# Value steps applied to the head outputs, and gated biases prepared in the projections

## The chip, the cores and the metric

The kernel runs on one core of one Trainium2 chip. A core has a matrix engine (TensorE, PE in the profile), a vector engine (VectorE, DVE), a scalar engine (ScalarE, ACT), a general one (GpSimd, POOL) and a sync engine (SyncE, SP), which here does nothing but issue DMAs. Each engine takes its own instructions in order, and the engines wait for one another on semaphores. The metric is device time in microseconds (us), taken over one execution of the whole program.

## The reference

`x` is 4 x 512 rows of 512 numbers (2048 rows in all, 16 tiles of 128), the context is 4 x 1024 rows (4096 rows, 32 tiles). All query rows see all context rows: the batch is folded into one.

```
x = x + tanh(g_xattn) * xattn(layernorm(x), ctx)
x = x + tanh(g_ffn)   * ffn(layernorm(x))

xattn: q = xn @ Wq + bq ; k, v = ctx @ Wkv + bkv          (16 heads of 32)
       q, k rounded to 8-bit integers, one step for each row and head
       v rounded to 8-bit integers, one step for each column of v:  v = vint * sv[column]
       p = softmax(q k^T / sqrt(32)), rounded to 0..255, one step for each row
       o = p @ v ;  y = o @ Wp + bp
ffn:   two layers with ternary weights on 8-bit rows, silu, gelu and a layernorm between; bias b1, b2
```

`sv` has one number for each of the 512 columns of `v`, that is for each (head, column of the head). The columns of `o` are the rows of `Wp`, so the factor `sv` can be put on `v`, on `o` or on the rows of `Wp`. The tests draw biases that are not zero.

## The kernel before

**The projections** (the first 235 us or so). 48 steps, one for each row tile: 32 of the context and 16 of `x`, in an order written out by hand (`order`). A step turns a tile on TensorE, multiplies it by the weights and rounds the rows on VectorE. Beside them a dictionary `extra` holds work that is hung on a step number: the gates' loads (step 5), their `tanh` (step 45, `gates`), the loading of the FFN weights in eight pieces through two buffers of the pool `wr` (`piece_load`, `piece_sum`, `piece_ternary`, `piece_store`), and `b1` (steps 22 and 23). GpSimd has little to do here. SP issues every load and store of this stage in order.

**The attention.** 256 units, one for each (head, tile of 128 query rows). In unit i TensorE makes 4096 scores for each row, VectorE multiplies them by the keys' steps out of PSUM into a buffer and takes the row maximum, in three chunks of 1536, 1536 and 1024 (`scores`, line 731; a, b and c below). Then `exps(i)` runs: two tiny GpSimd instructions join the three maxima (`m`, line 746) and make the bias (`nb`, line 748), and ScalarE makes the exponentials as bytes (`r`, line 751). A DMA transposes `r` (`turn_exps`, line 765), GpSimd spreads the bytes to 16 bits in two casts for each unit (`rT`, line 785), and TensorE multiplies them with the integers of `v` (line 801). After four units of a head ScalarE takes the sum out of PSUM (`leave`, line 812) and its own queue stores it to `ods` (line 813). Program order puts `scores(i+1)`'s first chunk ahead of `exps(i)`.

There are three score buffers up to unit 237 (`TWO`); one of them, `third`, is then given up and holds `Wp` (`wp_sb`), the biases `bp` and `b2` (`vecs`) and `b1`. From there on two buffers are left, so that chunk a of unit i+2 can only start when `exp(i)` is done.

A dictionary `plan` holds work hung on (unit, place in the unit). The values of head groups 1, 2 and 3 (`plan_group`) are made inside the attention, in units 3 to 63, 64 to 128 and 129 to 193. The last heads' units also start the output projection: `load_for_ffn` at unit 239 loads `Wp` and the biases into `third`; GpSimd then puts the gate on `bp` (`vector_for_ffn`, line 190), the values' steps on the four blocks of `Wp` (`projection_step`, line 281), adds `bp` to the first two tiles of `x` (`bias_x`, line 1001) and puts the gate on `b2`. Tile 0 has its softmax steps widened on ScalarE (`wide_step`, line 1014) and turned on TensorE at unit 242, multiplied with `o` on VectorE at 243 (`scale_o`, line 1036), projected with `Wp` from 243 to 247 (`first_project`, line 1404) and added to `x` at 247 (`residual_x`, line 1049). Tile 1 does the same from unit 248 on.

**The FFN** (from 1450 us or so). Tiles go in pairs; each turn of the pipeline has TensorE, ScalarE, VectorE and GpSimd on different pairs. `bias_x` adds `bp` to the later tiles of `x`, and `bias_y` adds `b2`.

Of the kernel before, what the change touches and what calls it, by code (L numbers as in the profile page):

```python
# [33 lines left out]
def flamingo_kernel(  # L34
# [124 lines left out]
    }  # L159
    b1r = third[:, at_vecs + 8 * C : at_vecs + 8 * C + 2 * INNER].bitcast(BF16)  # L160
    b1d = dram.tile([3, INNER], BF16, name="b1d")

    def load_b1(pool):
        bf = pool.tile([IC, P], F32, name="bf", bufs=1)
# [11 lines left out]

    def load_for_ffn():
        nc.sync.dma_start(wp_sb, wp.rearrange("(c p) n -> p c n", p=P))
        for name, v in (("bp", bp), ("b2", b2)):
            nc.sync.dma_start(vecs[name], row(v, C))  # L180
        for r in range(2):
            for a in range(3):
                at = r * HD + 3 * a
                nc.sync.dma_start(
                    b1r[at : at + 3, :].rearrange("p (m n w) -> p m n w", n=2, w=512)[:, :, r, :],
                    b1d.rearrange("p (m n w) -> p m n w", n=2, w=512)[:, :, r, :],
                )

    def vector_for_ffn(name, tg):
        nc.gpsimd.tensor_scalar(vecs[name], vecs[name], tg, 0.0, ALU.mult, ALU.add)  # L190

    def key_tile(n):

# [82 lines left out]
            vqs[g] = vqp.tile([P, KT, P], F16, name="vq")  # L276
        nc.sync.dma_start_transpose(vqs[g][:, j * VB : (j + 1) * VB, :], vh)

    def projection_step(g):

        nc.gpsimd.tensor_scalar(
            wp_sb[:, g, :], wp_sb[:, g, :], sv[:, g : g + 1], 1.0 / INT_STEP, ALU.mult, ALU.mult
        )

    def integers(pool, f, scale):

# [21 lines left out]
    with tc.tile_pool(name="pw", bufs=1) as pw, tc.tile_pool(  # L308
# [215 lines left out]
            partial(nc.sync.dma_start, bq_sb, row(bq, C)),  # L524
        ]
        extra[5].append(load_gates)
        extra[45].append(gates)
        extra[4] += [partial(nc.vector.tensor_scalar, bq_sb, bq_sb, QSCALE, None, ALU.mult)]
        for j in range(8):
            extra[6 + 2 * j].append(partial(piece_load, j))  # L530
# [9 lines left out]

        extra[22].append(ffn_load)
        extra[23].append(lambda: parts_of_b1(pieces.pop(0), wr))
        LASTK = KT + QT - END - 1
        for k, n in ((-6, 0), (-3, 4), (-1, 5), (1, 1), (1, 2), (1, 3)):
            extra[LASTK + k].append(partial(load_piece, 0, n))
# [87 lines left out]
    def plan_group(g, u0, dense):  # L633
        wv_g = wvs.next()
        vmx = fs.tile([P, KT // VB], F32, name="vmx")
        state = {}

        def start(j):
            return u0 + 3 * j - min(j, dense)

        def values(b):
            if b in (0, 5, 6, 7):
                return vgs[b % 4]
            if g not in vqs:
                vqs[g] = vqp.tile([P, KT, P], F16, name="vq")
            at = (b - 1) * VB * P
            return vqs[g].rearrange("p a b -> p (a b)").bitcast(F32)[:, at : at + VB * P]

        def load(j):
            cT = cTs.next()  # L650
            b, a = divmod(j * VW, VB * P)
            nc.sync.dma_start(cT, cTd[b][:, :, a : a + VW])
            state["cT", j] = cT

        def product(j, c):
            if c == 0:
                state["acc"] = aav.tile([P, 512], F32, name="vacc")[:, :VW]
            nc.tensor.matmul(  # L658
                state["acc"], wv_g[:, c, :], state["cT", j][:, c, :],
                start=(c == 0), stop=(c == CC - 1),  # L660
            )

        def leave(j):
            b, a = divmod(j * VW, VB * P)
            nc.scalar.activation(  # L665
                values(b)[:, a : a + VW],
                state.pop("acc"),
                AF.Identity,
                bias=bv[:, g : g + 1],
            )  # L670
            state.pop(("cT", j))

        def largest(b):
            nc.vector.tensor_reduce(
                vmx[:, b : b + 1], values(b), AX.X, ALU.max, apply_absolute_value=True
            )

        def integer(j):
            state["vi", j] = value_integers(vis.next(), g, values(j))

        def cast(j):
            state["vh", j] = vhs.next()
            nc.vector.tensor_copy(state["vh", j], state.pop(("vi", j)))

        def turn(j):
            values_by_key(state.pop(("vh", j)), g, j)

        nc.sync.dma_start(wv_g, values_weight(g))
        load(0)
        for j in range(NV):  # L690
            u = start(j)
            v = start(j + 1) - 1
            for c, place in enumerate(((u, 2), (u + 1, 0), (v, 0) if v > u + 1 else (v, 1), (v, 2))):
                plan[place].append(partial(product, j, c))
            if j + 1 < NV:
                plan[u, 1].append(partial(load, j + 1))
            plan[v, 2].append(partial(leave, j))
            if (j + 1) * VW % (VB * P) == 0:
                plan[v + 1, 1].append(partial(largest, j * VW // (VB * P)))
        u = start(NV)  # L700
        plan[u + 1, 0].append(partial(value_scale, g, vmx))
        for k, j in enumerate((1, 0, *range(2, KT // VB))):
            n = u - 1 + 2 * k
            plan[n + 3, 0].append(partial(integer, j))
            plan[n + 4, 2].append(partial(cast, j))
            plan[n + 5, 1].append(partial(turn, j))
# [65 lines left out]
    def plan_values(i, h, tg):  # L772

        pTs = [heads.pop(("p", h, tg * TG // 2 + u)) for u in range(TG // 2)]
        acc = aav.tile([P, 512], F32, name="acc")[:, :P]
        vq = vqs[h // HPG]
        NW = KT // 2 // 4
        spreads = {}  # L780

        def spread(k, u, cast=nc.gpsimd.tensor_copy):
            if u == 0:
                spreads[k] = at.tile([P, TG, 2 * NW, P], F16, name="rT")
            cast(  # L785
                spreads[k][:, 2 * u : 2 * u + 2, :, :]
                .bitcast(I16)
                .rearrange("p a (two b) q -> p a two (b q)", two=2),
                pTs[u][:, :, k * NW : (k + 1) * NW, :]
                .rearrange("p a b q -> p a (b q)")  # L790
                .bitcast(U8)
                .rearrange("p a (n two) -> p a two n", two=2),
            )

        def products(k):
            rT = spreads.pop(k)
            for b in range(2 * NW):
                two, w = divmod(b, NW)
                kb = at_tile[two * KT // 2 + k * NW + w]
                for c in range(TG):  # L800
                    nc.tensor.matmul(  # L801
                        acc[c * HD : (c + 1) * HD, :],
                        vq[:, kb, h % HPG * HD : (h % HPG + 1) * HD],
                        rT[:, c, b, :],
                        start=(k == 0 and b == 0),
                        stop=(k == 3 and b == 2 * NW - 1),
                        tile_position=(0, c * HD),
                    )

        def leave():  # L810
            o = ar.tile([P, P], F32, name="o", bufs=2)
            nc.scalar.copy(o, acc)
            nc.scalar.dma_start(
                ods[tg][h * HD : (h + 1) * HD, :].rearrange("d (c q) -> c d q", c=TG), o
            )

        for k in range(4):
            for u in range(TG // 2):

                unit = i + 4 + k  # L820
                if unit < len(steps):
                    place = unit, 0
                else:
                    place = unit - 1, 2 + (unit == len(steps))
                plan[place].append(partial(spread, k, u))
            plan[i + 5 + k, 1].append(partial(products, k))
        plan[i + 8, 2].append(leave)
# [159 lines left out]
        return range(g * GT, (g + 1) * GT)  # L987

    def load_x(t):
        nc.sync.dma_start(X[t], x[t * P : (t + 1) * P, :])  # L990

    def load_o(t):
        o = fm["o"].next()
# [16 lines left out]
    def wide_step(t):  # L1010

        step_w = fm["step_w"].next()
        step = ff.pop(("step", t))
        nc.scalar.copy(step_w, step.unsqueeze(2).to_broadcast([P, H, HD]))
        ff["step_w", t] = step_w

    def bias_y(g):
# [381 lines left out]
    def first_project(t, n):  # L1399
# [6 lines left out]
            start=(k == 0), stop=(k == NG - 1),  # L1406
        )

    for j in range(8):
        a = j * INNER // 8  # L1410
        at_unit(
            199 + 3 * j, 1,
            partial(
                nc.sync.dma_start_transpose,
                w1T[:, :, a : a + INNER // 8],
                w1q[a : a + INNER // 8, :],
            ),
        )
    at_unit(TWO + 2, 0, load_for_ffn)
    at_unit(TWO + 3, 2, partial(vector_for_ffn, "bp", tg1))  # L1420
    for g in range(NG):
        at_unit(TWO + 4 + g // 2, 1, partial(projection_step, g))
    at_unit(TWO + 7, 1, partial(vector_for_ffn, "b2", tg2))
    at_unit(
        TWO + 7, 1,
        partial(
# [5 lines left out]
    for t in range(2):  # L1432
        at_unit(240, t, partial(load_x, t))
        at_unit(241, 1, partial(load_o, t))
        at_unit(242 + t, 0, partial(bias_x, t))
    at_unit(241, 0, partial(steps_x, 0))
    for t, u in ((0, 242), (1, 248)):
        at_unit(u - 1, 2, partial(wide_step, t))
# [181 lines left out]
```

## Time and profile before

| | |
|---|---|
| median of 3 runs | 1698.74 us (1696.87 to 1700.41) |
| the profiled execution | 1701.51 us |
| its span in the trace | 1699.7 us |
| instructions | 31473 |
| granted TensorE clock, mean | 0.651 of full speed |
| mean DMA rate | 178 GB/s |

Busy time counts the instructions of an engine, not its waits. The stages differ: TensorE is busy for nine tenths and more of the projections, VectorE for nearly all of the attention, with GpSimd not far behind, and no engine alone fills the FFN. So a change is read in the stage where it lies. The chain that ended last leads back through casts on GpSimd (8% of the span), score chunks on VectorE (3%) and many small links.

In the lines below the first number is the start in us from the start of the span and the second the duration, or the span of a merged group; what stands in square brackets is the idle time of the engine just before, and what ended it.

### The profile page before, as it was taken

The page shows a single profiled execution, that of the slowest core. Times are in us where ns is not written, and L with a number is a line of the kernel's source. Part 1 is how long each engine was busy: PE and PEld are TensorE (multiplying, and loading weights), DVE is VectorE, ACT ScalarE, POOL GpSimd, SP SyncE. Part 2 cuts the span into 40 slices and gives each one's busy share as a digit, 9 for nine tenths or more (in the row PEclk, how much of TensorE's full clock was granted, in tenths as well). Part 3 has the DMA queues.
Part 4 walks back from the last instruction along what each step waited for, and adds up shares of the span by engine and source line. Part 5 has one row for each costly group of instructions (what it writes and reads, how often), then busy time and mean ns, then how long its engine had stood idle before and what let it go on. Part 6 is the DMA issues. An engine that isn't in the chain of part 4 may idle for free. (4 is left out here: it accounts for less than half of the span.)

```text
span 1699.7 us, 31473 instructions
## 1 busy us (share of the span) xinstructions
PE 1352.5 (80%) x12174; PEld 589.7 (35%) x12174; DVE 1564.2 (92%) x2205; ACT 1346.5 (79%) x988; POOL 1284.0 (76%) x1315
## 2 busy tenths in 40 slices
PE   8999968888966889986689898666665676789986
PEld 4444423333322333332233333222222233334432
DVE  5787889999999999999999999999999989588987
ACT  2443468888889888888988888898887876679987
POOL 0001226999999999999989999999999998566645
PEclk9999975565555555565555555555555556899998
DMA  6767969999999999998899999889999776613325
GB/s 210 273 249 249 295 196 222 196 212 207 159 180 171 217 178 209 199 170 177 158 211 185 207 197 178 180 151 189 173 183 174 153 139 128 171 43 87 93 50 117
DMA packets 729418, 303.32 MB, mean 178 GB/s; under 512 B 657266, under 2 KB 702902, under 8 KB 722870
## 3 DMA queue, kind: packets, MB, share of 16 engines
q1 hardware_dynamic: 720502, 296.60, 81.6%
q10 hardware_dynamic: 8736, 4.72, 1.1%
q8 instruction: 95, 1.56, 0.4%
q14 instruction: 53, 0.43, 0.1%
q0 software_dynamic: 32, 0.01, 0.0%
HBM read 103.86 MB, written 33.83 MB: 81 GB/s over the span
## 5 line engine op out<-in xcount | busy, mean ns | idle before, releaser
L785 POOL CAST rT<-pT 128x2048 int16<-128x2048 uint8 x506 | 944.5, 1893 | 22.9 <-issue 5.6
L731 DVE CUSTOM_DVE_ANT_0 s<-ps_s,skb 128x1536 f32<-128x1536 f32 x531 | 805.6, 1574 | 15.3 <-PE ps_s L722 7.5
L751 ACT ACTIVATE r<-s,nb,sq 128x4096 uint8<-128x4096 f32 x177 | 673.8, 3807 | 118.3 <-POOL nb L748 96.2
L722 PE MATMUL ps_s<-kT,qT 32*128 32x512 bf16 x2048 | 458.3, 585 | 264.5 <-DVE m L731 250.1
L731 DVE CUSTOM_DVE_ANT_0 third<-ps_s,skb 128x1536 f32<-128x1536 f32 (+1 forms) x237 | 362.6, 1574 | 3.8 <-ACT r L751 1.3
L751 ACT ACTIVATE r<-third,nb,sq 128x4096 uint8<-128x4096 f32 x79 | 300.7, 3806 | 47.8 <-POOL nb L748 35.9
L722 PEld LDWEIGHTS <-qT 32*128 32x128 bf16 x2048 | 97.7, 98 | 591.0 <-issue 581.9
L801 PE MATMUL acc<-rT,vq 128*32 128x128 f16 x8192 | 262.6, 305 | 19.4 <-POOL rT L785 9.9
L801 PEld LDWEIGHTS <-vq 128*32 128x32 f16 x8192 | 195.4, 137 | 131.5 <-issue 106.9
L658 PE MATMUL vacc<-fx 128*128 128x256 f32 x384 | 227.8, 695 | 2.6 <-ACT vq L665 1.9
L746 POOL TENSOR_SCALAR m<-m 128x1 f32<-128x1 f32 x256 | 91.9, 359 | 60.4 <-DVE m L731 50.7
L471 POOL TENSOR_SCALAR nsq<-sq 128x16 f32<-128x16 f32 x16 | 3.2, 203 | 171.7 <-DVE sq L290 171.7
L658 PEld LDWEIGHTS vacc<-fx 128*128 128x128 f32 x384 | 93.5, 302 | 83.9 <-issue 80.5
L430 PE MATMUL kacc<-wk_sb,cT 128*128 128x512 f32 x256 | 117.6, 603 | 0.0
L748 POOL TENSOR_SCALAR nb<-m,nsq 128x1 f32<-128x1 f32 x256 | 68.0, 266 | 23.9
L1113 PE MATMUL ph<-fx,skb 128*128 128x512 bf16 x256 | 63.6, 393 | 0.1
L430 PEld LDWEIGHTS kacc<-wk_sb,cT 128*128 128x128 f32 x256 | 47.1, 194 | 47.6 <-issue 46.9
L731 DVE DVE_READ_ACCUMULATOR2_ANT m<- 128x1 f32 x768 | 63.0, 82 | 0.0
L430 PE MATMUL qacc<-wq_sb,xT 128*128 128x512 f32 x128 | 59.4, 608 | 0.1
L459 DVE TENSOR_TENSOR f<-kacc,bk_sb 128x512 f32<-128x512 f32 x32 | 22.0, 689 | 30.9 <-PE kacc L430 29.9
L299 ACT COPY cT<-tr 128x512 f32<-128x512 f32 x32 | 18.6, 581 | 34.6 <-PE tr L298 34.4
L359 POOL TENSOR_SCALAR wi<-wt 128x512 bf16<-128x512 int32 (+1 forms) x32 | 21.7, 703 | 31.5 <-ACT wt L355 31.5
(236 smaller groups left out, 1365.4 us busy)
## 6 DMA issues: line engine op xcount, KB each, us to landing
skb<-skd SPq DMA_DIRECT2D x32, 1024.0 KB
fx<-cTd SPq DMA_DIRECT2D x48, 512.0 KB
wt<-in_L_ffn_w_dram SPq DMA_DIRECT2D x16, 1024.0 KB
in<-in_ctx_dram SPq DMA_DIRECT2D x32, 256.0 KB
cTd<-cT SPq DMA_DIRECT2D x8, 1024.0 KB
q4d<-rows4q SPq DMA_DIRECT2D x16, 512.0 KB
pT<-r SPq DMA_TRANSPOSE x260
in<-in_x_dram SPq DMA_DIRECT2D x16, 256.0 KB
```

Of the source, the lines that this page charges most:

```text
L359: nc.gpsimd.tensor_scalar(wi[:, a : a + w4], wt.bitcast(I32)[:, a : a + w4], 1.0, -1.0, ALU.min, ALU.max)
L430: nc.tensor.matmul(acc, tT[:, c, :], wk_sb[c] if kind == "k" else wq_sb[:, c, :], start=(c == 0), stop=(c == CC - 1),)
L459: nc.vector.tensor_tensor(f, acc, bk_sb, ALU.add)
L658: nc.tensor.matmul(state["acc"], wv_g[:, c, :], state["cT", j][:, c, :], start=(c == 0), stop=(c == CC - 1),)
L722: nc.tensor.matmul(ps_s[:, b * KB - k0 : (b + 1) * KB - k0], qT[rows, 0, t * P : (t + 1) * P], kT[rows, 0, a * KB : (a + 1) * KB], start=True,
L731: nc.vector.tensor_tensor_reduce(s[:, k0 : k0 + w], ps_s[:, :w], skb[:, k0 : k0 + w], 1.0, -3.0e38, ALU.mult, ALU.max, m3[:, n : n + 1],)
L746: nc.gpsimd.tensor_scalar(m, m3[:, 0:1], m3[:, 1:2], m3[:, 2:3], ALU.max, ALU.max)
L748: nc.gpsimd.tensor_scalar(nb, m, nsq[:, t, h : h + 1], LN255, ALU.mult, ALU.add)
L751: nc.scalar.activation(r.rearrange("p (n two) -> p two n", two=2), s.rearrange("p (two n) -> p two n", two=2), AF.Exp, bias=nb, scale=sq[: ...
L785: cast(spreads[k][:, 2 * u : 2 * u + 2, :, :] .bitcast(I16) .rearrange("p a (two b) q -> p a two (b q)", two=2), pTs[u][:, :, k * NW : (k ...
L801: nc.tensor.matmul(acc[c * HD : (c + 1) * HD, :], vq[:, kb, h % HPG * HD : (h % HPG + 1) * HD], rT[:, c, b, :], start=(k == 0 and b == 0), ...
L1113: nc.tensor.matmul(ph[:, n, :], xqT[:, c, tok], w1T[:, c, at : at + 512], start=(c == 0), stop=False,)
```

## The change

The step `sv` is no longer multiplied onto `Wp`. It is stored to memory for each group of four heads and read back with the head's column as the partition, repeated for the four row tiles that share the PSUM tile (`svr`); `leave` multiplies by it while it takes a sum out of PSUM. The constant that went with it is put on in `wide_step`. The gates' `tanh` is taken at step 9 of the projections instead of step 45. The two biases are gated there, added to the first two tiles of `x`, and stored to memory (`xbd`, `gbd`); later loads read these.

```diff
-        for name, v in (("bp", bp), ("b2", b2)):
-            nc.sync.dma_start(vecs[name], row(v, C))
+        for k, name in enumerate(("bp", "b2")):
+            nc.sync.dma_start(vecs[name], gbd[k : k + 1, :].broadcast_to([P, C]))
...
-    def vector_for_ffn(name, tg):
-        nc.gpsimd.tensor_scalar(vecs[name], vecs[name], tg, 0.0, ALU.mult, ALU.add)
...
-    def projection_step(g):
-
-        nc.gpsimd.tensor_scalar(
-            wp_sb[:, g, :], wp_sb[:, g, :], sv[:, g : g + 1], 1.0 / INT_STEP, ALU.mult, ALU.mult
-        )
+    svr = keep.tile([P, H], F32, name="svr")
+    svd = dram.tile([NG, P], F32, name="svd")
+
+    def store_scale(g):
+        nc.sync.dma_start(svd[g : g + 1, :].rearrange("a p -> p a"), sv[:, g : g + 1])
+
+    def load_scale(g):
+        for c in range(HPG):
+            nc.sync.dma_start(
+                svr[c * HD : (c + 1) * HD, g * HPG : (g + 1) * HPG],
+                svd[g : g + 1, :].rearrange("a (h d) -> (a d) h", d=HD),
+            )
...
-        extra[45].append(gates)
+        extra[9].append(gates)
...
+        def bias_load():
+            wt = wr.tile([P, INNER], F32, name="wt")
+            biased.append(wt)
+            for k, v in enumerate((x[:P, :], x[P : 2 * P, :], row(bp, C), row(b2, C))):
+                nc.sync.dma_start(wt[:, k * C : (k + 1) * C], v)
+
+        def bias_steps():
+            wt = biased[0]
+            for k, tg in ((2, tg1), (3, tg2)):
+                b_k = wt[:, k * C : (k + 1) * C]
+                nc.gpsimd.tensor_scalar(b_k, b_k, tg, 0.0, ALU.mult, ALU.add)
+            for k in range(2):
+                for a in range(0, C, P):
+                    x_k = wt[:, k * C + a : k * C + a + P]
+                    nc.gpsimd.tensor_tensor(x_k, x_k, wt[:, 2 * C + a : 2 * C + a + P], ALU.add)
+
+        def bias_store():
+            wt = biased.pop()
+            nc.sync.dma_start(
+                xbd.rearrange("(a p) c -> p a c", p=P),
+                wt[:, : 2 * C].rearrange("p (a c) -> p a c", c=C),
+            )
+            nc.sync.dma_start(
+                gbd.rearrange("(a k) c -> a k c", a=1),
+                wt[:1, 2 * C :].rearrange("p (a c) -> p a c", c=C),
+            )
+
+        for k, f in ((21, bias_load), (22, bias_steps), (24, bias_store)):
+            extra[k].append(f)
...
+        plan[u + 2, 2].append(partial(store_scale, g))
+        plan[u + 5, 2].append(partial(load_scale, g))
...
-            nc.scalar.copy(o, acc)
+            nc.scalar.activation(o, acc, AF.Identity, scale=svr[:, h : h + 1])
...
-        nc.sync.dma_start(X[t], x[t * P : (t + 1) * P, :])
+        src = xbd if t < 2 else x
+        nc.sync.dma_start(X[t], src[t * P : (t + 1) * P, :])
...
-        nc.scalar.copy(step_w, step.unsqueeze(2).to_broadcast([P, H, HD]))
+        nc.scalar.activation(
+            step_w, step.unsqueeze(2).to_broadcast([P, H, HD]), AF.Copy, scale=1.0 / INT_STEP
+        )
...
+    at_unit(5, 2, partial(store_scale, 0))
+    at_unit(8, 0, partial(load_scale, 0))
...
-    at_unit(TWO + 3, 2, partial(vector_for_ffn, "bp", tg1))
-    for g in range(NG):
-        at_unit(TWO + 4 + g // 2, 1, partial(projection_step, g))
-    at_unit(TWO + 7, 1, partial(vector_for_ffn, "b2", tg2))
...
-        at_unit(242 + t, 0, partial(bias_x, t))
```

For group 0 the step is stored at unit 5 and read back at unit 8. For groups 1, 2 and 3 `u` is 50, 114 and 179, so it is stored at units 52, 116 and 181 and read back at 55, 119 and 184.

More of the change, by code (lines that the diff above doesn't have):

```diff
@@ L161, in flamingo_kernel @@
     b1d = dram.tile([3, INNER], BF16, name="b1d")
+    gbd = dram.tile([2, C], F32, name="gbd")
+    xbd = dram.tile([2 * P, C], F32, name="xbd")
     def load_b1(pool):
@@ L542, in flamingo_kernel @@
         extra[23].append(lambda: parts_of_b1(pieces.pop(0), wr))
+        biased = []
+        def bias_load():
[24 more added lines that the diff above has]
+            extra[k].append(f)
         LASTK = KT + QT - END - 1
```

## The prediction

> **What bounds the kernel now.** I read the page's slices first, then busy time by windows of 40 us, then the timeline at each place that an edit touches.
>
> ```profile
> DVE  5787889999999999999999999999999989588987
> POOL 0001226999999999999989999999999998566645
> ...
> 80.00:120.00 40.00, 39.66 (x122) 19.03 (x121) 29.90 (x64) 21.91 (x38) 3.70 (x9) 1.00 0.66 232
> 280.00:320.00 40.00, 35.14 (x376) 15.22 (x364) 39.18 (x52) 33.77 (x22) 37.09 (x34) 0.50 1.09 215
> 1200.00:1240.00 40.00, 25.30 (x360) 10.68 (x360) 40.00 (x55) 34.89 (x21) 38.59 (x37) 0.50 1.01 180
> 1360.00:1400.00 40.00, 28.96 (x297) 12.86 (x292) 34.51 (x48) 29.70 (x19) 38.44 (x38) 0.54 0.75 138
> ```
>
> After each window come the busy us of PE, its weight loads, DVE, ACT and POOL, then clock, DMA share and GB/s. Projections: PE has 39.7 of 40 us and is the bound. Attention: DVE has all of it (4.48 us of score chunks for each unit), POOL follows with 4.50 us from one `m` to the next. One place stands out: 1360 to 1400, where DVE falls to 34.5 and POOL does not. There the timeline, without PE, reads:
>
> ```profile
> 1367.33 3.73 POOL L785 CAST rT<-pT 128x2048 int16<-128x2048 uint8 x2
> 1369.97 1.76 DVE L731 CUSTOM_DVE_ANT_0 s<-ps_s,skb 128x1536 f32<-128x1536 f32 x1 [0.69 <-ACT r L751]
> 1371.04 1.36 POOL L281 TENSOR_SCALAR third<-third,sv 128x512 f32<-128x512 f32 x2
> 1372.39 0.35 POOL L746 TENSOR_SCALAR m<-m 128x1 f32<-128x1 f32 x1
> 1373.13 3.81 ACT L751 ACTIVATE r<-s,nb,sq 128x4096 uint8<-128x4096 f32 x1 [3.20 <-POOL nb L748]
> 1377.06 1.76 DVE L731 CUSTOM_DVE_ANT_0 s<-ps_s,skb 128x1536 f32<-128x1536 f32 x1 [1.91 <-ACT r L751]
> ```
>
> The scaling of `Wp` sits ahead of `m` in POOL's order, the exponential waits 3.20 us for POOL, and with two score buffers DVE waits 1.91 us for the exponential. So here, and only here, POOL's order sets the pace.
>
> **What the change removes.** Six 128x512 TENSOR_SCALARs on POOL (two gated biases of 0.69, four blocks of `Wp` in pairs of 1.36) and two `bias_x` (1.29 and 1.28): 1.38 + 2.72 + 2.57 = 6.67 us, all between 1358 and 1384. They do not come back in full, because DVE is next. I followed the units by four rules, each read off this stretch. An exponential ends 3.92 us after it starts. It starts 0.75 us after `m` starts. `m` starts 0.11 after DVE's chunk c, or 4.49 after the `m` before it (two casts between). Chunk a of unit i+2 needs DVE free, `exp(i)` ended and its PE scores. Starts of exp, before and after:
>
> - exp(240): 1360.20 to 1359.53 (POOL is free of casts at 1358.77; the gated bias of 0.69 is gone).
> - exp(241): 1366.04 to 1364.62. DVE's chunk c still ends at 1363.75; only the 1.36 of POOL is gone.
> - exp(242): 1373.13 to 1369.51. Chunk b waits until 1365.75 for PE, which turns the softmax steps first; chunk c ends at 1368.65.
> - exp(243): 1378.88 to 1374.64 (`scale_o` adds 0.60 to DVE).
> - exp(244): 1384.29 to 1380.06. With POOL out of the way, PE's projection is late next: it comes between two score chunks. Tile 1 shows it, with no POOL extras: 2.06 us from chunk c (1407.31) to the next chunk a (1409.37), of which DVE idles 0.83, and 0.31 more at 1414.27.
> - exp(245): 1388.78 to 1384.95; then chunk a of unit 247 comes at 1388.95 instead of 1392.72.
>
> That is a gain of 3.75 us, and from there on the order is as before. Bounds: comparing the six exponentials after 241 (32.87 us) with tile 1's six after 247 (30.19) gives 2.7; if PE's 0.83 + 0.31 did not return, 4.9.
>
> **What it adds in the attention: the value steps.** For each group one store and four loads on SP. Rows for small transfers:
>
> ```profile
> L585 SPq DMA_DIRECT2D bv<-in_L_xattn_bkv_dram x1: 435/435/435, 9.3 to 9.3; - x1
> L184 SPq DMA_DIRECT2D third<-b1d x6: 685/686/867, 1349.2 to 1353.6; - x6
> 259.55 4.94 SPq L765 DMA_TRANSPOSE pT<-r  x1
> 290.38 3.81 ACT L751 ACTIVATE r<-s,nb,sq 128x4096 uint8<-128x4096 f32 x1 [1.63 <-DMA pT<-r]
> 301.48 3.81 ACT L751 ACTIVATE r<-s,nb,sq 128x4096 uint8<-128x4096 f32 x1 [1.89 <-DMA pT<-r]
> ```
>
> SP's issue is 0.44 to 0.87 us each, so 2.2 to 4.3 for five. The 640 numbers of 4 bytes, at the mean packet of the queue (81.6% of 16 x 1699.7 us over 720502 packets = 31 ns) on 16 engines, take 1.2 us. The transposes are queued behind them, and behind the transposes `r`'s buffers and ACT. Group 0 falls on units 5 to 8, where DMA is full (share 1.09) and ACT already waits for transposes. DVE has cover: exp(11) ends at 299.5 and DVE needs its buffer at 301.88, 2.4 us. Lateness of 2.2 (issue alone) costs 0; of 5.5 (both at their highest) 3.1. The row nearest in kind is `bv`, also numbers of 4 bytes: 5 x 0.44 + 1.2 = 3.4, so I take 1.0. For groups 1 to 3 (units 52, 116, 181 on) ACT waits for no transpose, and its exponentials end some 4.2 us before DVE needs the buffer (three units of 4.5 less 4.5 for the chunks, 0.86 and 3.92): 0, at most 1.3 each if the lateness were 5.5. The store is two units and more ahead of its load, so I take no wait there.
>
> The Trainium skill speaks against this transfer: DMA: Bandwidth & Descriptors, section Rules for kernel authors, says that a last dimension which is not contiguous becomes one descriptor for each element and should be rearranged. Taken at its word it says to avoid this, but it prices nothing; the number above is from the queue's own packets. No run here shows the 4-byte load yet.
>
> **ACT.** `leave` is a COPY now and becomes an ACTIVATE with an operand for each partition.
>
> ```profile
> L812 ACT COPY o<-acc x64: 241/244/259, 294.2 to 1492.8; 128x128 f32<-128x128 f32 x64
> L452 ACT ACTIVATE fx<-vacc,bv x8: 688/689/689, 29.8 to 234.6; 128x512 f32<-128x512 f32 x8
> L299 ACT COPY cT<-tr x32: 564/587/587, 5.7 to 208.8; 128x512 f32<-128x512 f32 x32
> 224.12 1.28 ACT L104 ACT_TABLE_LOAD   x1
> 115.12 0.63 PE L298 MATMUL tr<-ident,in 128*128 128x128 f32 x4 [0.22 <-DVE in L413]
> ```
>
> From 0.587 to 0.689 is 0.10 us; 64 times that is 6.5 us of ACT, in the attention under the 4.2 us cover. The 16 `wide_step`s take a constant: 0, at most 0.10 each. In the FFN ACT is busy 37.6 of 40 us, so of 13 wide steps and the last `leave`s I take 0.2 in all, 0 to 1.6. If the cover in the attention were gone it would be the 6.5.
>
> **The projections.** `tanh` at step 9 costs two loads of a function table more (1.28 each): one for `tanh`, one for the next square root; the load at 224 moves to the first exponential. At step 9 ACT's next needed copy (57.15) is 3 us ahead of PE's use (61.08). At step 12 the copy at 70.95 ends 1.44 us before PE's use (72.95): cover for 1.28. The first exponential comes 1.28 later; it ended at 248.26 and DVE needed its buffer at 250.05, a cover of 1.8. I take 0.1; uncovered it would be 3.8.
>
> On SP: six more DMAs (1.5 MB), 0.44 us each; rows are loaded five steps (20 us) ahead. The store at step 24 waits for POOL, and loads of rows and an FFN piece queue behind it. POOL's steps: 2 x 0.69 and eight adds of 128x128, between a quarter of 1.28 and the 0.73 of a 16x128 add in this stage, 4 to 7 us from 113 on, so done by 120 at the latest; SP gets to that store at 116 to 120. That is inside the load's lead: 0, and the buffer is free again by the piece at step 27. POOL's work beside DVE slows DVE a little (the normalising pass takes 0.64 beside POOL's cast, 0.55 alone), and PE already waits 0.22 for that pass at step 23. I take 0.2, 0 to 3 (if four DVE passes each waited for a whole POOL instruction of 0.73).
>
> The page ScalarE: Activation LUTs of the skill, section What ACT_TABLE_LOAD costs, adds a drain of about 1.38 us to each load, 2.66 in all. In this trace the copy before the load at 224.12 ends at 224.10 and the `tanh` starts at 225.41, so no drain is seen. By the page the step-12 cover of 1.44 would fail by 1.2 us, and the sum below would be -1.05 instead of -2.25.
>
> **Sum.** -3.75 + 1.0 + 0.2 + 0.1 + 0.2 = -2.25 us. On the profiled execution's 1701.51 that is 1699.3; that execution lies 2.8 us above the median of the runs (1698.74), which on the median is 1696.5, 0.13% faster.
>
> **Rivals.**
>
> 1. *The covers hold whole.* The value steps cost nothing, as lateness under 2.4 us does. For: DVE waits for ACT nowhere between 262 and 320 now, although ACT waits for DMA five times. Against: those five waits show the DMA full. Gain 3.75 to 4.9: 1693.8 to 1695.0, around 1694.7.
> 2. *The gain is eaten.* PE's projections hold DVE as in tile 1 (gain 2.7), and the value steps (up to 3.1) with the projections' share make up for it. For: DVE waits for PE in tile 1. Against: unit 241's part of the gain does not depend on PE. About 1698.7.
> 3. *Slower: the small transfers hold up the transposes.* If each of the five DMAs in units 5 to 8 held the queue as long as the slow transposes (4.94 us), `r` would be 24.7 late; less 2.4 of cover, 22 us, against 3.75: 1717. It decides from a lateness of 2.4 + 3.75 + 3.4 = 9.6 us on: past that the kernel is over 0.2% slower. For: 4-byte packets have no row under load. Against: `bv` was issued in 0.44 us.
>
> **How the numbers follow.** 0.2% is 3.4 us, about what a measurement of this kernel can tell. The forecast (a gain of 0.8 to 3.4) has 0.40, rival 1 0.33, rival 2 0.13, rival 3 0.14. Faster by over 0.2% is rival 1: 0.33; within it the forecast and rival 2: 0.53; slower rival 3: 0.14. The range goes from rival 1's best (1693.8) up to the lower gain with the value steps, ACT and 1.0 in the projections at their bounds: 2.7 - 3.1 - 1.6 - 1.0 = -3.0, so 1701.7. It leaves out the worse part of rival 3 and little at the lower end. The forecast's own range is 1695.3 to 1698.0.
>
> **What would show it.** Right: no POOL TENSOR_SCALAR on `third` after 1350; the exponential of unit 242 no longer waits 3.20 us for `nb`; chunks there wait for PE instead; POOL's busy time in the attention's last 60 us down by 6.7. `leave` at 0.34. ACT_TABLE_LOADs near 57 and 68, none at 224. In 262 to 320 ACT's waits for `pT` longer by 1 to 3 us, DVE's by 1. Wrong: DVE waiting for `r` early in the attention by more than 3 us, PE below 39 of 40 us at 60 to 130, or exp(239) to exp(246) still taking 38 us.

## The result, and the profile after

The changed kernel takes 1704.88 us, the median of 6 runs (1701.73 to 1710.66), beside 1700.51 us for the kernel before (6 runs). The ratio is 1.0035 with a 95% interval of 1.0024 to 1.0046: slower, where no measurable change was forecast. The profiled execution took 1703.82 us, with a span of 1701.8 us.

To see where the time went I compare, unit by unit, the start of VectorE's first score chunk (chunk a) in the two traces. VectorE works in order and fills the attention, so this start is the clock of the stage. After minus before, in us:

```
unit      0      8      9     14     24     40     72    144    184    192    241    244    246    247    255
after  -0.57  -0.34  +2.72  +4.71  +6.46  +6.95  +6.96  +5.32  +4.97  +6.25  +6.00  +4.20  +2.46  +2.82  +2.82
```

The gain at the change of tiles (units 241 to 247) is there: +6.00 falls to +2.82, 3.2 us. But 7.3 us had been lost before, between units 8 and 40, where only group 0's steps are new. Some of it comes back between 72 and 184, and 1.3 us go in one step at unit 185, behind group 3's store (unit 181).

**The loss.** These lines of the timeline of the kernel after follow the store of group 0's steps. SPq is the sync engine's DMA queue.

```profile
264.95 0.53 SPq L282 DMA_DIRECT2D svd<-sv  x1
265.58 1.92 SPq L805 DMA_TRANSPOSE pT<-r  x1
267.56 1.02 SPq L690 DMA_DIRECT2D fx<-cTd  x1
268.67 8.07 SPq L805 DMA_TRANSPOSE pT<-r  x1
...
275.53 3.81 ACT L791 ACTIVATE r<-s,nb,sq 128x4096 uint8<-128x4096 f32 x1 [5.60 <-DMA pT<-r]
279.34 0.46 ACT L703 ACTIVATE fx<-vacc,bv 128x256 f32<-128x256 f32 x1
279.82 0.69 DVE L712 TENSOR_REDUCE vmx<-fx 128x1 f32<-128x512 f32 x1 [2.77 <-ACT fx L703]
280.51 2.19 SPq L286 DMA_DIRECT2D svr<-svd  x4
290.53 3.81 ACT L791 ACTIVATE r<-s,nb,sq 128x4096 uint8<-128x4096 f32 x1 [3.16 <-DMA pT<-r]
294.34 0.46 ACT L703 ACTIVATE vq<-vacc,bv 128x256 f32<-128x256 f32 x1
296.77 1.76 DVE L771 CUSTOM_DVE_ANT_0 s<-ps_s,skb 128x1536 f32<-128x1536 f32 x1 [1.25 <-PE ps_s L762]
300.94 1.23 DVE L771 CUSTOM_DVE_ANT_0 s<-ps_s,skb 128x1024 f32<-128x1024 f32 x1 [0.73 <-PE ps_s L762]
```

The same work in the timeline of the kernel before, in the same order:

```profile
268.96 3.57 SPq L765 DMA_TRANSPOSE pT<-r  x1
...
270.65 3.79 ACT L751 ACTIVATE r<-s,nb,sq 128x4096 uint8<-128x4096 f32 x1
274.44 0.46 ACT L665 ACTIVATE fx<-vacc,bv 128x256 f32<-128x256 f32 x1
277.31 0.68 DVE L674 TENSOR_REDUCE vmx<-fx 128x1 f32<-128x512 f32 x1
```

The store itself is issued in 0.53 us. The second transpose behind it is where the time goes: 8.07 us on the queue instead of 3.57. The exponential that needs its buffer starts at 275.53 instead of 270.65, 4.88 us late. Behind that exponential in ScalarE's order stands the eviction of the next group's values (`fx`), and VectorE's maximum over them (`vmx`) waits for it: 2.77 us of VectorE lost directly, where 2.4 us had been to spare (274.90 to 277.31). At 296.77 and 300.94 VectorE then waits for TensorE, 1.25 and 0.73 us. TensorE had waited for two evictions of ScalarE, of `vq` (1.48 us) and of the head's sum (`leave`, 1.02 us), and these stand behind exponentials again; the one at 290.53 waits 3.16 us for a transpose. Both lie behind the four loads at 280.51, but the loads need not be the cause: see the runs with stores alone and loads alone.

What happened at 268 shows in windows of 2 us, first after, then before (columns as in the prediction's windows; the last is GB/s):

```profile
268.00:270.00 2.00, 2.00 (x9) 0.61 (x6) 2.00 (x3) 1.94 (x2) 0.90 (x3) 0.50 2.35 152
270.00:272.00 2.00, 2.00 (x8) 0.91 (x6) 2.00 (x3) 0.00 (x0) 1.61 (x1) 0.50 0.31 12
272.00:274.00 2.00, 2.00 (x10) 0.47 (x10) 1.73 (x5) 0.00 (x0) 0.00 (x0) 0.50 0.87 92
```

```profile
268.00:270.00 2.00, 2.00 (x9) 0.71 (x8) 2.00 (x5) 2.00 (x1) 0.62 (x2) 0.50 1.07 198
270.00:272.00 2.00, 2.00 (x7) 0.60 (x4) 2.00 (x3) 2.00 (x3) 1.94 (x3) 0.50 1.07 276
272.00:274.00 2.00, 2.00 (x10) 0.72 (x8) 1.73 (x5) 2.00 (x1) 2.00 (x2) 0.50 1.05 225
```

DMA moves 12 GB/s instead of 276 from 270 to 272. Packets hang: between 269.98 and 271.70 no packet starts at all, while some 20 are under way. The trace's packets of 2.5 us and more in the changed kernel, all of them (the four stores' own packets are at 266, 485, 783 and 1089 us):

```
start us       packets   bytes            longest us
269.4-272.4       9      1024                3.49
486.7-488.5      19      256, and 16384      3.60
788.1-788.8      21      256 and 512         3.34
1091.7-1094.6     6      256                 3.31
```

The kernel before has two such packets in the whole run (both at 538, 2.58 us at most). The one of 16384 bytes, at 486.7, belongs to an instruction queue, and those of 512 bytes to ScalarE's: the pause is not confined to the queue on which the store was issued.

The waits of 240 to 345, after and before (us in total, times, longest), sum the effect on ScalarE:

```profile
ACT r L791 <- DMA pT<-r: 17.0, 7, 5.6
```

```profile
ACT r L751 <- DMA pT<-r: 7.2, 5, 2.1
```

**The gain.** The timeline of the kernel after at the change of tiles, exponentials and the VectorE chunks that waited:

```profile
1361.03 3.81 ACT L791 ACTIVATE r<-s,nb,sq 128x4096 uint8<-128x4096 f32 x1 [0.72 <-POOL nb L788]
1366.25 3.81 ACT L791 ACTIVATE r<-s,nb,sq 128x4096 uint8<-128x4096 f32 x1 [1.32 <-DMA pT<-r]
1370.61 3.81 ACT L791 ACTIVATE r<-s,nb,sq 128x4096 uint8<-128x4096 f32 x1
1376.19 3.81 ACT L791 ACTIVATE r<-s,nb,sq 128x4096 uint8<-128x4096 f32 x1 [1.68 <-POOL nb L788]
...
1381.26 1.76 DVE L771 CUSTOM_DVE_ANT_0 s<-ps_s,skb 128x1536 f32<-128x1536 f32 x1 [0.84 <-PE ps_s L762]
1386.16 1.76 DVE L771 CUSTOM_DVE_ANT_0 s<-ps_s,skb 128x1536 f32<-128x1536 f32 x1 [0.31 <-PE ps_s L762]
```

These are exp(239) to exp(242). The wait of exp(242) for `nb` is 1.68 us instead of 3.20, and VectorE's waits there are for TensorE (0.84 and 0.31) and, at 0.29 and 0.42, for ScalarE. From exp(239) to exp(246) it is 35.1 us (1361.03 to 1396.11) instead of 38.6.

The lines that answer to the others shown of before, from the page (VectorE's and GpSimd's slices) and from the windows of 40 us:

```profile
DVE  5787888999999999999999999999999999578988
...
POOL 0021225999999999999999999999999888656645
```

```profile
80.00:120.00 40.00, 39.81 (x119) 18.85 (x118) 30.78 (x65) 21.59 (x38) 3.81 (x9) 1.00 0.76 251
240.00:280.00 40.00, 24.11 (x113) 7.45 (x109) 35.87 (x49) 31.61 (x22) 13.62 (x24) 0.50 0.94 164
280.00:320.00 40.00, 33.59 (x342) 14.16 (x342) 36.85 (x49) 31.80 (x21) 34.72 (x33) 0.50 0.96 210
1360.00:1400.00 40.00, 28.56 (x340) 13.02 (x339) 37.38 (x51) 32.21 (x21) 35.04 (x33) 0.59 0.83 149
```

VectorE's busy time in 280 to 320 is 36.85 us (39.18 before), and in 1360 to 1400 it is 37.38 (34.51 before): the loss and the gain side by side, although the second window lies six us earlier in the work.

### The profile page after: what moved, and what is told of

It reads as the page before. It is cut to its first block, busy times and chain, and to the rows that moved or that the text cites. A ratio compares the mean times of both kernels' runs of the same rounds, so it can differ in the third digit from the quotient of the medians.

```text
span 1701.8 us, 31519 instructions
## 1 busy us (share of the span) xinstructions
PE 1354.3 (80%) x12174; PEld 589.6 (35%) x12174; DVE 1565.2 (92%) x2205; ACT 1354.2 (80%) x990; POOL 1279.8 (75%) x1317
```

## The experiments

Each ratio is to the kernel before on the same chip, with its 95% interval. A change of 0.001 is 1.7 us. Starts of chunk a are given against the kernel before, as above; a single profile can slip by 3 to 4 us somewhere by itself, as two of them show below, so verdicts go by ratios.

**Are the transfers the loss?** The first kernel of the series has the whole change but no store and no load of the steps (`svr` is set to 1, so the scaling is left out):

```diff
+    nc.vector.memset(svr, 1.0)
     def store_scale(g):
-        nc.sync.dma_start(svd[g : g + 1, :].rearrange("a p -> p a"), sv[:, g : g + 1])
+        pass
     def load_scale(g):
-        for c in range(HPG):
...
+        pass
```

> The changed kernel without the four stores and sixteen loads of the value steps; `svr` holds ones, so the outputs of the heads keep the wrong scale and that part is left out. Theory A (the small transfers hold up the transposes at the start of the attention): the delay of chunk a against the kernel before, 5.2 us at unit 20 and 7.0 at unit 40 in the changed kernel, is under 1 us; the gain of 3.2 us between units 242 and 247 stays; the projections stay 0.5 earlier; time ratio to before 0.9975 to 0.9985. Theory B (the slower `leave` on ScalarE, or the early function tables, cost the time): the delay at unit 40 stays at 5 us or more and the ratio over 1.002.

Measured: 1695.65 us, ratio 0.9981 (0.9972 to 0.9991). Chunk a stands at +1.54 us at unit 40, +0.17 at 80, -0.35 at 241 and -3.37 at 255. So the rest of the change gains some 3 us, and the transfers cost 1.0035 less 0.9981, 0.0054, or 9 us. The forecast of the other parts was -3.25. One thing is not as expected: chunk a is +0.55 us at unit 8 already and +1.54 at unit 40, so some 1.0 us is lost between these units without any transfer of the steps.

**The store or the loads?** One kernel keeps the stores alone, one the loads alone (with `svd` filled in the projections by one store of whole rows):

```diff
 # stores only: svr is set to 1.0
     def load_scale(g):
-        for c in range(HPG):
...
+        pass
 # loads only
     def store_scale(g):
-        nc.sync.dma_start(svd[g : g + 1, :].rearrange("a p -> p a"), sv[:, g : g + 1])
+        pass
...
+        extra[30].append(partial(nc.sync.dma_start, svd, ones[:NG, :]))
```

> The changed kernel with the four stores of the value steps, without the loads (`svr` holds ones; the scaling is left out). Theory A1 (the store of 128 numbers of 4 bytes to one row of memory stalls all DMA for some 4 us): chunk a is 3 us late at unit 9 as in the changed kernel, and packets of over 2.5 us follow each store within 6 us; by unit 40 some 3 to 5 us late. Theory A2 (the loads do it): under 1 us late at unit 40 and no such packets.

> The changed kernel with the sixteen loads at their places, while the memory that they read is written once in the projections, by four rows of 512 bytes (all ones; the scaling is left out). Theory A1 (the stores stall the DMA): chunk a under 2 us late at unit 40, no packets of over 2.6 us. Theory A2 (the loads do it, 2.2 us of SyncE and 512 descriptors in the fullest stretch): 3 us or more late at unit 40, from unit 10 on.

Measured: stores alone 1702.07 us, ratio 1.0014 (1.0004 to 1.0024); loads alone 1698.77, ratio 0.9998 (0.9988 to 1.0008). Against the kernel without transfers the stores cost 0.0033 and the loads 0.0017 (each to about 0.0014); together 0.0050 of the 0.0054. With stores alone the wait behind the store of group 0 is the changed kernel's, as its timeline shows:

```profile
275.52 3.80 ACT L788 ACTIVATE r<-s,nb,sq 128x4096 uint8<-128x4096 f32 x1 [5.27 <-DMA pT<-r]
...
279.81 0.69 DVE L709 TENSOR_REDUCE vmx<-fx 128x1 f32<-128x512 f32 x1 [2.85 <-ACT fx L700]
...
300.15 1.23 DVE L768 CUSTOM_DVE_ANT_0 s<-ps_s,skb 128x1024 f32<-128x1024 f32 x1 [1.29 <-PE ps_s L759]
```

and its packets of 2.5 us and more lie again behind the four stores (269 to 272, 485, 787 and 1093 to 1095; up to 3.21 us). With loads alone there are none. The second loss of the changed kernel, 1.25 and 0.73 us at unit 12, is not the loads' alone: at the same unit VectorE waits 1.29 us for TensorE with stores alone and 0.53 with loads alone. Between units 8 and 40 chunk a loses 6.0 us with stores alone (-0.44 to +5.60), 2.7 with loads alone (-1.98 to +0.76), 1.0 with neither and 7.3 with both. So the larger part is the store, which the prediction had costed at its issue and nothing else.

**What about the store?** A store writes 128 numbers of 4 bytes, one from each partition, side by side into one row of 512 bytes. The first attempt put five kinds of small transfer into quiet units (222 to 234) of the kernel before: such a store, the same column copied on chip, a column stored 2048 bytes apart, one whole row, and four loads.

```diff
+    at_unit(222, 2, partial(nc.sync.dma_start, one_row[:1, :].rearrange("a p -> p a"), col))
+    at_unit(225, 2, partial(nc.sync.dma_start, pr[:, 8:9], col))
+    at_unit(228, 2, partial(nc.sync.dma_start, far_rows[:, 0:1], col))
+    at_unit(231, 2, partial(nc.sync.dma_start, whole_row, ones[:1, :]))
+    at_unit(234, 2, probe_loads)
```

> The kernel before with five probes of the DMA, 13 us apart, in the quiet end of the attention: at unit 222 the store as in the change (128 numbers of 4 bytes into one row of 512 bytes), at 225 the same column copied inside the on-chip memory, at 228 the same store with 2 KB between the numbers, at 231 one row of 512 bytes, at 234 the four loads. If many small writes into one place of memory stall it: packets of over 2.5 us and some 4 us of low DMA rate after the first alone. If every transfer of single numbers does: after the first, second, third and last. If it is any write to memory of a small size: after the first, third and fourth. If it was only the full queue of units 5 to 8: nowhere.

Measured: 1698.64 us, one run. No packet of 2.5 us follows any of the five. After the store at 1266 us DMA falls to 35 GB/s over 4 us at 1271, but the kernel before falls to 44 over 4 us at 1278 in the same work. This run settles nothing: DMA moves less there (137 GB/s from 1264 to 1284 in the kernel before, against 195 at 260 to 280, 210 at 480 to 500, 223 at 783 to 803 and 191 at 1084 to 1104, all over 20 us), so it can't say what the store does in the change's own places.

So the next kernel is the change in place, with each number in a row of its own, 512 bytes from the next. Number of packets, bytes and issues are the same:

```diff
-    svd = dram.tile([NG, P], F32, name="svd")
+    svd = dram.tile([NG, P, P], F32, name="svd")
...
-        nc.sync.dma_start(svd[g : g + 1, :].rearrange("a p -> p a"), sv[:, g : g + 1])
+        nc.sync.dma_start(svd[g, :, 0:1], sv[:, g : g + 1])
...
-                svd[g : g + 1, :].rearrange("a (h d) -> (a d) h", d=HD),
+                svd[g, :, 0].rearrange("(h d) -> d h", d=HD),
```

> The whole change, but each of the 128 numbers of a store goes to its own place, 512 bytes from the next; as many packets as in the change, and the loads read them there. Theory M1 (many small writes into one row of 512 bytes are served one by one, and reads of memory wait): no stall of 4 us after the stores, no packets of over 2.6 us, ratio as with the loads alone, 0.999 to 1.001. Theory M2 (any 128 small writes to memory stall the reads behind them): stalls as in the change, ratio 1.002 to 1.0045.

Measured: 1699.67 us, ratio 0.9999 (0.9990 to 1.0007): the same as with loads alone, and 0.0036 under the changed kernel. The timeline of this kernel at group 0's store:

```profile
262.92 0.53 SPq L282 DMA_DIRECT2D svd<-sv  x1
263.55 1.90 SPq L805 DMA_TRANSPOSE pT<-r  x1
265.50 1.03 SPq L690 DMA_DIRECT2D fx<-cTd  x1
266.62 3.44 SPq L805 DMA_TRANSPOSE pT<-r  x1
```

The transpose that took 8.07 us takes 3.44. No packet of 2.5 us follows any of its four stores. (There is one such group, at 286 us, 10 us after the loads, behind which VectorE waits 3.77 us in this profile; a similar one comes in two other kernels below where no small transfer is near.) So it is the writing of many small pieces side by side, not the number of small packets. The Trainium skill, DMA: Bandwidth & Descriptors, section Specifications, says that transfers below 512 bytes are done by reading, changing and writing back. This fits a cost for small writes, but by itself it does not tell the two layouts apart, since both write 4 bytes at a time. That writes into the same 512 bytes have to wait for one another, and reads behind them, would explain it; no run here shows the inside of the memory, so this stays argued. Nor is it shown that only memory is concerned: the hung packets of 256 bytes are on a queue that is mostly filled with transposes from one on-chip tile to another (`pT<-r`).

**The steps without memory.** Four heads of 32 columns lie in one column of `sv`. Sixteen matmuls of one column with slices of the identity put them where `leave` needs them, and one copy of 128x4 on ScalarE (0.138 us) takes them out:

```diff
+    def spread_scale(g):
+        ps_v = aav.tile([P, 512], F32, name="vacc")[:, :HPG]
+        for h in range(HPG):
+            for c in range(HPG):
+                nc.tensor.matmul(
+                    ps_v[c * HD : (c + 1) * HD, h : h + 1], ident[:, h * HD : (h + 1) * HD],
+                    sv[:, g : g + 1], start=True, stop=True, tile_position=(0, c * HD),
+                )
+        nc.scalar.copy(svr[:, g * HPG : (g + 1) * HPG], ps_v)
...
-        plan[u + 2, 2].append(partial(store_scale, g))
-        plan[u + 5, 2].append(partial(load_scale, g))
+        plan[u + 2, 2].append(partial(spread_scale, g))
...
-    at_unit(5, 2, partial(store_scale, 0))
-    at_unit(8, 0, partial(load_scale, 0))
+    at_unit(2, 2, partial(spread_scale, 0))
```

> The whole change, but `svr` is made by sixteen matmuls of 32 columns of the identity with the group's steps, and one copy out of PSUM, instead of the store and the four loads. Theory A (only the small transfers cost): as without them, ratio to the kernel before 0.9975 to 0.9990, chunk a under 1.5 us late at unit 40, a gain of 2.6 to 3.5 us between units 242 and 247. If it were something that comes with the scaling itself: over 1.001.

Measured: 1697.04 us, ratio 0.9984 (0.9973 to 0.9995), faster than the kernel before and the changed one. Its profiled execution slips 3.7 us between units 24 and 32, where 19 packets of 256 bytes take up to 3.18 us at 342.7; no small transfer is near, so such a pause can come by itself, and the 1.5 us expected for unit 40 are passed for this reason. At the change of tiles it gains 3.9 us (+2.65 at unit 241, -1.24 at 247), above the 2.6 to 3.5 expected, and its six exponentials after that run as the prediction had them: set against the start of exp(239), exp(240) to exp(245) lie 0.67, 1.44, 3.67, 4.31, 4.30 and 3.88 us earlier than before, for a forecast of 0.67, 1.42, 3.62, 4.24, 4.23 and 3.83. It is the best case: the eight profiled kernels with both parts gain 2.6 to 3.9 us there (mean 3.1), and in six of them exp(240) waits 0.8 to 1.5 us for a transpose.

**The two halves alone,** each on the kernel before: the biases (gates at step 9, biases made in the projections, `xbd` and `gbd`), and the value steps with the matmuls above.

```diff
 # biases only: as in the change; projection_step stays on Wp
-    at_unit(TWO + 3, 2, partial(vector_for_ffn, "bp", tg1))
-    at_unit(TWO + 7, 1, partial(vector_for_ffn, "b2", tg2))
-        at_unit(242 + t, 0, partial(bias_x, t))
 # steps only: leave and wide_step as in the change, spread_scale; biases stay
-        at_unit(TWO + 4 + g // 2, 1, partial(projection_step, g))
+    at_unit(2, 2, partial(spread_scale, 0))
```

> The kernel before with the bias part of the change alone: gates at step 9, biases and two tiles of x made in the projections; the scaling of `Wp` on GpSimd stays. It takes 3.95 of the 6.67 us from GpSimd. If GpSimd's order alone sets the pace there, 3.5 to 4 us come back; by the units followed in the prediction, 1.5 to 2.5 (exp(240) 0.67, one `bias_x` of 1.28 in unit 242, the other partly under PE's wait). Ratio 0.9980 to 0.9995. Projections within 0.6 us of the kernel before.

> The kernel before with the value steps in `leave` alone, spread by matmuls, the bias part left as before: 2.72 of the 6.67 us leave GpSimd. If its order alone set the pace, 2.7 us come back; with PE's projection late next, 1 to 2.5. Ratio 0.9985 to 0.9998. If the two parts share one slack, the gains of this run and of the biases alone add up to more than the 3.2 us of both together; if each is limited on its own, to about that.

Measured: biases alone 1696.46 us, ratio 0.9977 (0.9967 to 0.9986); steps alone 1697.58, ratio 0.9985 (0.9976 to 0.9993). The two gains add up to 0.0038, more than the 0.0016 of both together (the difference is 0.0022, known to about 0.0017). At the change of tiles they gain 3.1 and 2.7 us; both together gain 2.6 to 3.9, as said above, and not the 5.8 of the sum. Neither half was expected to return so much (1.5 to 2.5 and 1 to 2.5): of the 2.72 us that the steps take from GpSimd all comes back. The two parts cut the same wait. Past either of them VectorE meets the next one, 0.83 us for TensorE or for the eviction of a sum, as in the changed kernel (0.84). So one half is enough by what these runs can tell, and which of these three versions is the fastest can't be told: their intervals overlap.

**Where do the transfers cost?** The last pair sends the steps of group 0 alone, or those of groups 1 to 3 alone, through memory as in the change, and spreads the others by matmul.

```diff
 # group 0 by memory
-        plan[u + 2, 2].append(partial(store_scale, g))
-        plan[u + 5, 2].append(partial(load_scale, g))
+        plan[u + 2, 2].append(partial(spread_scale, g))
 # groups 1 to 3 by memory
-    at_unit(5, 2, partial(store_scale, 0))
-    at_unit(8, 0, partial(load_scale, 0))
+    at_unit(2, 2, partial(spread_scale, 0))
```

> The whole change, but only group 0's steps go through memory (one store at unit 5, four loads at unit 8); the steps of groups 1, 2 and 3 are spread by 16 small matmuls each and one copy on ScalarE. Theory A (the transfers cost time in group 0 alone, because units 3 to 40 have no cover there): some 6 us of the 7 lost in units 8 to 40 come back on DVE's chunks here too, and the time is that of the whole change less about 1: ratio to the kernel before 1.0015 to 1.0035. Theory B (the loss is spread evenly over the four groups, and the profile of one execution misleads): a quarter of 0.0051, so ratio 0.9990 to 1.0003.

> The whole change, but group 0's steps are spread by matmuls at unit 2 and only groups 1, 2 and 3 go through memory (stores at units 52, 116 and 181, loads three units on). Theory A (group 0 alone costs): DMA still nearly stops after the three stores near 485, 788 and 1092, but DVE loses at most 1.3 us there; ratio 0.9980 to 0.9995, like the version with no transfer of the steps (0.9984). Theory B (the loss is spread evenly): three quarters of 0.0051, so ratio 1.0015 to 1.0030.

Measured: group 0 by memory 1702.68 us, ratio 1.0021 (1.0012 to 1.0030); groups 1 to 3 by memory 1698.28, ratio 0.9990 (0.9980 to 1.0000). Against the version with none in memory group 0 costs 0.0037, or 6 us, the other three together 0.0006, which can't be told from nothing. In the first, chunk a goes from -0.85 us at unit 8 to +5.97 at unit 40. In the second the pauses are there and as deep; these are its windows after the store of group 3 (packets at 1085 us):

```profile
1084.00:1086.00 2.00, 1.29 (x30) 0.61 (x19) 2.00 (x3) 2.00 (x1) 2.00 (x2) 0.50 1.13 301
1086.00:1088.00 2.00, 1.02 (x6) 0.20 (x5) 2.00 (x5) 2.00 (x3) 2.00 (x2) 0.50 1.74 98
1088.00:1090.00 2.00, 1.79 (x37) 0.98 (x35) 2.00 (x3) 2.00 (x2) 1.84 (x3) 0.50 1.21 7
1090.00:1092.00 2.00, 0.61 (x3) 0.10 (x3) 2.00 (x5) 2.00 (x1) 2.00 (x2) 0.50 0.66 48
```

DMA falls to 7 GB/s, single packets take up to 5.24 us, and VectorE is busy for the whole of every window. Behind the three stores ScalarE's exponentials wait 1.81, 2.26 and 1.43 us for a transpose, and VectorE waits nowhere for 0.2 us or more: so much of the cover of 4.2 us that the prediction gave to groups 1 to 3 is real. Chunk a of this kernel stands at +0.33 us at unit 184 and +0.36 at 192. (It slips 3.5 us between units 24 and 32, with 18 packets of up to 3.33 us at 339 us and no small transfer near, as did the version without any.)

## Why the prediction was wrong

**The term that failed is "what it adds in the attention: the value steps", 1.0 us with bounds of 0 and 3.1.** Measured, it is 0.0051 to 0.0054 of the time, 9 us, of which group 0 has 6 by itself. With 9 in place of 1.0 the sum of -2.25 becomes +5.75, and the ratio of 1.0035 is 6 us.

The form of the term was right, its size was not. It was lateness less cover. The cover of 2.4 us was found at the score buffers; in the runs VectorE met the late exponential earlier, at the maximum of the values behind the eviction `fx`, where the slack was also 2.4 us. The lateness was taken as five issues of 0.44 us and the packets' own time, 3.4 us. The store's packets are short and its issue is 0.53 us, but some four us later other transfers' packets hang for up to 3.5 us and one transpose takes 4.5 us longer. The nearest row taken (`bv`) was a load, 9 us from the start of the program, and only its issue was read. It was issued beside other traffic (DMA moved 389 GB/s from 9 to 11 us), but it is a load and not a store. Neither `bv` nor the mean packet of the queue (31 ns) could show what a store does to its neighbours. The sentence that "the store is two units and more ahead of its load, so I take no wait there" looked for a wait in the wrong place: not at the load of the same numbers, but at every transfer behind the store.

**Rival 3** said this in its direction, "small transfers hold up the transposes", with a threshold of 9.6 us of lateness. The loss of 7.3 us between units 8 and 40, of which some 1.0 also comes without any transfer, makes 8.7 to 9.7 with the 2.4 of cover, about there. Its picture was different: five transfers holding the queue 4.94 us each. It is one pause behind the store (3.1 us of VectorE), then waits for TensorE and for evictions that come in part with the store alone. The chance of 0.14 was too low for a cost that no row bounded; so was the upper end of the range, which left rival 3 out. That end also left out bounds which the text itself had given: 1.3 us for each of groups 1 to 3, and 3 instead of 1.0 for the projections. With them it would have been 1707.6 instead of 1701.7 and would have held the 1704.88, though not for the reason that the runs show.

**The rule that was set aside.** The Trainium skill, DMA: Bandwidth & Descriptors, section Rules for kernel authors, speaks against a last dimension that is not contiguous. It was right that these transfers should be avoided, though its reason (one descriptor for each element) does not separate the store that costs from the store 512 bytes apart that doesn't.

**Groups 1 to 3** at 0, at most 1.3 each: right, 0.0006 in all, known to about 0.0015. The changed kernel's own profile loses 1.3 us at unit 185, where TensorE waits for `leave` behind a late exponential.

**The gain of 3.75**, between 2.7 and 4.9: the mechanism is right, the size a little high. It is 3.2 us in the changed kernel, where exp(240) waits 1.32 us for a transpose, 3.1 in the mean of the eight profiles with both parts (2.6 to 3.9), and 3.9 with the steps spread by matmuls, the one profile in which all six exponentials lie within 0.07 us of their forecast. The four rules had no wait for a transpose. "PE's projection is late next" shows in the waits of 0.84 and 0.31 us, beside the 0.83 and 0.31 read off tile 1.

**ACT.** These group lines of the changed kernel are from the views of the tiles `svr` and `svd` (minimum, median and maximum in ns; first and last start):

```profile
L852 ACT ACTIVATE o<-acc,svr x64: 345/350/365, 298.9 to 1495.6; 128x128 f32<-128x128 f32 x64
L286 SPq DMA_DIRECT2D svr<-svd x16: 418/430/1141, 280.5 to 1106.3; - x16
L282 SPq DMA_DIRECT2D svd<-sv x4: 369/536/541, 264.9 to 1085.8; - x4
```

`leave` takes 0.350 us for 0.244, as predicted (0.34), and no cost of it shows: with the value steps alone and no transfer, chunk a loses nothing between units 8 and 40. The issues of 0.43 and 0.54 us were right too, and were not the cost.

**The tables.** The timeline of ScalarE after:

```profile
55.72 1.28 ACT L104 ACT_TABLE_LOAD   x1
...
65.18 1.28 ACT L411 ACT_TABLE_LOAD   x1
...
242.46 1.28 ACT L791 ACT_TABLE_LOAD   x1
243.89 3.81 ACT L791 ACTIVATE r<-s,nb,sq 128x4096 uint8<-128x4096 f32 x1
```

They are where the text put them, with none at 224. No cost shows: the square root's load ends before its operand comes (its ACTIVATE at 68.09 still waits 1.63 us for VectorE), and the first exponential, behind the third load, had waited 1.45 us for its bias before. It starts 0.57 us earlier than before (244.46), as the first score chunk does.

**The projections** at 0.2: GpSimd's block takes 5.54 us (116.80 to 122.34, where 4 to 7 was said, but done by 122, not 120), and TensorE keeps 39.81 of 40 us at 80 to 120. The first chunk comes 0.57 us earlier than before. Among the profiles with this part the first chunk lies between -2.9 and +0.5 us, among those without it between -3.1 and 0, so a cost of 0.2 can't be told.

## What to carry to other kernels

A store can cost more than its issue and its bytes, as the one of 128 small pieces into one row did here: ask what other transfers run in the next five us or so, and whether an engine without slack waits for one of them. When no row of the profile shows a transfer of the kind, under the load in which it will run, its upper bound is not the slowest issue; keep the range open until a run has shown it, or move the numbers another way, as sixteen tiny matmuls and a 0.14 us copy did here. And look for the cover at every instruction that stands behind the late one on its engine, not only at its main reader.

## What was not expected of the hardware

- In every one of the twelve stores of 128 times 4 bytes into one row of 512 bytes that ran in the attention's units up to 181 (4 in the changed kernel, 4 with stores alone, 1 and 3 in the last pair), packets of other transfers took 2.5 to 5.2 us within six us of the store's own packets, an instruction fetch among them. In none of the four stores with the numbers 512 bytes apart did they.
- The one such store in a quieter place (unit 222) was followed by none. What load on the DMA it takes was not tried.
- Pauses of the same look come now and then with no small transfer near (at 342.7 us and at 339 us in two profiles). Their cause stays open.
